# Relational graph convolution, gathered half: nine of a group's 18 edge tiles counted from its first edge, nine from its end

## The chip, the cores and the metric

The kernel runs on one core of one Trainium2 chip. The metric is the device time of one execution in microseconds (us), the median of several runs. "Edge tile" below means 128 consecutive edges; TensorE, VectorE, ScalarE, GpSimd and SyncE (SP, which issues most transfers) are the core's engines, in the profile PE, DVE, ACT, POOL and SP.

## The reference, cut to what matters

Two graph networks follow one another on N = 3125 nodes and E = 103125 edges, which are sorted by destination (50000 random edges, their reverses, and one loop for each node, so 33 edges a node on average).

```python
h = relu(layernorm(x));  x = x + gcn(h)          # 4 convolutions, hidden width 256
h = relu(layernorm(x));  x = x + rgcn(h)         # 3 layers, width 128, R = 16 relations

def rgcn_layer(x, src, tgt, edge_type, W, root, bias):
    seg = tgt * R + edge_type
    agg = segment_sum(x[src], seg, N * R)                     # a sum for each node and relation
    cnt = segment_sum(ones, seg, N * R)
    agg = agg / clip(cnt, 1)
    return einsum('nrd,rdo->no', agg, W) + x @ root + bias    # relu between layers
```

The change is in the second network: in how the edges of a node are brought to the sums `agg`.

## The kernel before, in words

The program has three parts.

**Index part** (`index_edges`). It packs each edge's destination, type and source in one word (`c_d`), finds by counting where each node's edges begin (`s_d`), and checks the assumptions that the rest rests on. The check ends in one flag (L618), on which all engines branch: to `regular`, or to a slow general path.

**First network.** Seven column blocks of an adjacency matrix (`adj_d`, q = 0 to 6, 512 nodes each) are built by TensorE, then multiplied with the features in four stages. In each stage `stream(q)` (L1205, on SP) loads a block and `aggregate` (L827) runs 75 or 150 matmuls over it; two buffers hold blocks. While this runs, smaller pieces of work that the second network needs are spread among the matmuls as generators. In the third such stage the generator is `relation_tiles` (steps taken in `between`), together with `residual` (L1327 to L1334) and `first_rows`, which finish x for the nodes of the block before.

**Second network** (`rgcn_mixed`). Nodes are handled in 25 blocks of 128, each for three layers. A block has two groups of GR = 64 nodes. The first half of a block takes its messages from features held on chip: one-hot matrices G (L1596) pick them with TensorE (L1621), ScalarE copies them out of PSUM (L1623), and matmuls with the one-hot S sum them by node and relation (L1688, L1692). The second half is the **gathered half**, group 2b + 1: GpSimd fetches the source rows with one indirect transfer for each edge tile (`msg`, L1518; 20 buffers), VectorE makes a one-hot `sel` from the tile's keys (L1637, six tiles an instruction), and TensorE multiplies (L1651), three times for each tile, since features are held as a sum of three bf16 terms. `plans` gives how many tiles go with each of a block's six batches; within a block these matmuls lie between those of the first half. VectorE scales the sums by 1 / cnt (`scaled`, L1512) into `gs`, and `project` (L1526, L1528) applies the relation weights.

A group has about 64 x 33 = 2112 edges. The kernel gives it TR = 18 tiles, which start at the group's first edge. Which nodes can occur in tile k isn't known when the program is built, so `windows` gives each tile an interval of nodes that its edges can belong to: where node n begins lies within five standard deviations of 33 n. The interval widens with the distance from the group's first edge. Its width sets the width of `sel` and the columns of L1651: (nodes in the window) x 16 relations. A group's sums lie in two PSUM tiles, one for 32 nodes each (half h = 0 and 1); a tile whose window crosses node 32 needs matmuls for both. `touched` lists the tiles of each half.

```python
found.append((lo, hi))             # windows(): node range of tile k, counted from the group's first edge
...
a0, a1 = max(lo, 32 * h), min(hi + 1, 32 * h + 32)       # rgcn_mixed: columns of half h
```

`relation_tiles` prepares this once. `gathered_words` loads every group's first edge number into `at` (L738, 18 small loads on SP, one for each tile), adds 128 k (L739) and fetches the words (`w`, L742, seven indirect transfers). `relative` makes node numbers relative to the group (L751, L752), L1241 subtracts the window's first node, and `to_edges` turns the results so that edges lie on partitions (L762, TensorE transposes), for the relative node `rel`, the type `typ` and the source. From these come the keys `key2` (L1248) and the sources `src_t` (L1251). Then one-hots `hr` and `ht` (L812) and small matmuls (L1275) count the edges by node and relation; these also use the windows.

The order of instructions on each engine is set when the program is built, by a scheduler that can move an instruction ahead of others that it doesn't depend on; what comes first in the program isn't always first on an engine.

Of the kernel before, what the change touches and what calls it, by code (L numbers as in the profile page):

```python
# [21 lines left out]
P = 128  # L22
N = 3125
# [19 lines left out]
GA, TA, CA = 8, 3, 13  # L43
RA = 32 * TA
IA = NB * GA
GR, TR, CR = 64, 18, 7
RR = 7 * TR
NGR = CR * 7
# [5 lines left out]
def windows(size, tiles):  # L54

    found = []
    for k in range(tiles):
        lo = max(n for n in range(size) if 33 * n + 5 * math.sqrt(32 * n) <= P * k)
        hi = min([n for n in range(size) if 33 * (n + 1) - 5 * math.sqrt(32 * (n + 1)) >= P * (k + 1)] + [size - 1])
        found.append((lo, hi))  # L60
    return found


def bounds(win, size, tiles):

    lows, highs = {}, {}
    for k, (lo, hi) in enumerate(win):
        highs[lo] = min(highs.get(lo, tiles * P), P * k)
        if hi < size - 1:
            lows[hi + 1] = max(lows.get(hi + 1, 0), P * (k + 1))  # L70
    return lows, highs


WIN = windows(GR, TR)
WINA = windows(GA, TA)


# [358 lines left out]
def index_edges(tc, keep, a, c_d, s_d, h_d, dinv, flag):  # L436


    nc = tc.nc
    with ExitStack() as x:  # L440
        prep = x.enter_context(tc.tile_pool(name="ix", bufs=1))
# [133 lines left out]

        wide = 2 * GR + 1
        g_i = prep.tile([NGR, GR + 1], I32, name="g_i")
        nc.sync.dma_start(g_i[:, :GR], s_d[: NGR * GR].rearrange("(g e) o -> g (e o)", e=GR))  # L580
        nc.sync.dma_start(g_i[:, GR:], s_d[GR: (NGR + 1) * GR].rearrange("(g e) o -> g (e o)", e=GR)[:, :1])
# [1 line left out]
        high = prep.tile([NGR, wide], F32, name="high")  # L583
        nc.vector.memset(low, 0.0)
        nc.vector.memset(high, float(TR * P))
        for o, step, size, (lows, highs) in ((0, GR, GR, bounds(WIN, GR, TR)),
                                              (GR + 1, GA, GR, bounds(WINA, GA, TA))):
            for t, values in ((low, lows), (high, highs)):
                for n, v in values.items():
                    nc.gpsimd.memset(t[:, o + n:o + size:step], float(v))  # L590
        g_f = prep.tile([NGR, wide], F32, name="g_f")
        nc.vector.tensor_copy(g_f[:, :GR + 1], g_i)
        nc.vector.tensor_copy(g_f[:, GR + 1:], g_i[:, :GR])
        g_r = prep.tile([NGR, wide], F32, name="g_r")
        nc.vector.tensor_scalar(g_r[:, :GR + 1], g_f[:, :GR + 1], g_f[:, :1], None, op0=ALU.subtract)
        g_e = g_f[:, GR + 1:].rearrange("p (g e) -> p g e", e=GA)
        nc.vector.tensor_tensor(g_r[:, GR + 1:].rearrange("p (g e) -> p g e", e=GA), g_e,
                                g_e[:, :, :1].to_broadcast([NGR, GR // GA, GA]), op=ALU.subtract)
        more = prep.tile([NGR, wide], F32, name="more")
        nc.vector.tensor_scalar(more, g_f, float(E), None, op0=ALU.is_lt)  # L600
# [40 lines left out]
def regular(ctx: ExitStack, tc: tile.TileContext, a: dict, out: bass.AP, c_d, s_d, h_d, dinv):  # L641
# [45 lines left out]
    with ExitStack() as gx:  # L687
# [24 lines left out]
        def gathered_words(pool, rows_, tiles, groups, cols, size):  # L712
# [12 lines left out]
            nc.vector.tensor_copy(k_f, k_i)  # L725
            p_f = pool.tile([n, 1], F32, name="p_f")
            nc.vector.tensor_copy(p_f, p_i)
            g_f = pool.tile([n, 1], F32, name="g_f")
            nc.vector.scalar_tensor_tensor(g_f, k_f, -float(groups), p_f, op0=ALU.mult, op1=ALU.add)
            nc.vector.tensor_scalar(g_f, g_f, float(size), None, op0=ALU.mult)  # L730
            nc.vector.tensor_scalar(k_f, k_f, float(P), None, op0=ALU.mult)
            base = pool.tile([n, cols], F32, name="base")
            iota(nc, base, [[size * groups, cols]])
            nc.vector.tensor_scalar(base, base, g_f, None, op0=ALU.add)
            at = pool.tile([n, cols], I32, name="at")
            first = s_d[: cols * groups * size].rearrange("(c g e) o -> g c (e o)", c=cols, g=groups)[:, :, 0]
            for k in range(tiles):
                nc.sync.dma_start(at[k * groups:(k + 1) * groups, :], first)  # L738
            nc.vector.tensor_scalar(at, at, k_f, None, op0=ALU.add)  # L739
            w = pool.tile([n, cols, P], I32, name="w")  # L740
            for c in range(cols):
                nc.gpsimd.indirect_dma_start(out=w[:, c, :], out_offset=None, in_=c_d,  # L742
                                             in_offset=bass.IndirectOffsetOnAxis(ap=at[:, c:c + 1], axis=0))
            return w, base

        def relative(pool, w, base):

# [474 lines left out]
        def relation_tiles():  # L1222

            with tc.tile_pool(name="tr", bufs=1) as tr:
                rel2 = tr.tile([P, CR * RR, 2], F16, name="rel2")
                typ2 = tr.tile([P, CR * RR, 2], F16, name="typ2")
                with tc.tile_pool(name="trw", bufs=1) as tw:
                    w, at = gathered_words(tw, RR, TR, 7, CR, GR)
                    yield

                    rel, d_i = relative(tw, w, at)
                    lo_f = tw.tile([RR, 1], F32, name="lo_f")
                    nc.vector.memset(lo_f, 0.0)
                    p_f = tw.tile([RR, 1], F32, name="pr_f")
                    iota(nc, p_f, [[0, 1]], 1)
                    more = tw.tile([RR, 1], F32, name="more")
                    for k in range(1, TR):
                        nc.vector.tensor_scalar(more, p_f, 7.0 * k, float(WIN[k][0] - WIN[k - 1][0]),
                                                op0=ALU.is_ge, op1=ALU.mult)
                        nc.vector.tensor_add(lo_f, lo_f, more)  # L1240
                    nc.vector.tensor_scalar(rel, rel, lo_f, 100.0, op0=ALU.subtract, op1=ALU.min)  # L1241
                    to_edges(tw, rel, RR, CR, dup(rel2, 1))
                    typ = tw.tile([RR, CR, P], F32, name="typ")
                    nc.vector.tensor_scalar(d_i, w, 12, NR - 1, op0=ALU.logical_shift_right, op1=ALU.bitwise_and)
# [496 lines left out]
```

## Time and profile before

| | |
|---|---|
| median of 3 runs | 2903.13 us (2902.95 to 2910.56) |
| profiled execution, its own time | 3358.47 us |
| its span, first to last instruction | 3356.6 us |
| second network, in the span | 1105 to 3357 us |
| PE busy, whole span | 2812.2 us (84%) |
| PE busy 1105 to 1815 us | 629.8 of 710 us |
| mean granted clock of TensorE | 0.935 |
| L1651 PE | 4536 matmuls, 10% of the chain of waits |
| L1518 POOL | 1296 gathers, 1051 ns each |
| L1637 DVE | 216 one-hots, 917 ns each |
| L738 SP, third stage | 18 loads in 6.38 us |

The profiled execution is 455 us longer than the median of the runs. Its durations are those of one execution; busy shares are averages over stages that differ, so each part of the work is to be looked up in its own stretch of the timeline. In a row of the groups of instructions, the numbers after the bar are busy us, mean ns of one, and the engine's idle time just before them, with what ended it. In a row of the timeline, the columns are start, us, engine, line, operation, out<-in, count, and in brackets the idle time before it.

### The profile page before, as it was taken

Reading aid. Unit: us, or ns where it says so; the run is one execution under the profiler, and the core shown is the slowest. Engines: PE = TensorE matmul, PEld = TensorE weight load, DVE = VectorE, ACT = ScalarE, POOL = GpSimd, SP = SyncE. Lnnn points to the kernel's source line nnn. Section 1 sums busy time; section 2 is a strip of 40 time slices with the busy share of each in tenths; the row PEclk is TensorE's granted clock in tenths of the full one; section 3 lists DMA queues with packets and bytes.
Section 4 is the critical chain, followed back from the end, with each engine's and each line's share of the span. In section 5 each row is a group of like instructions: output and inputs, shape, how many; then the busy total and the mean of one; then the engine's idle time right before and its main releaser. Section 6 shows DMA issues by size and latency. Waiting matters only on the chain.

```text
span 3356.6 us, 62945 instructions
## 1 busy us (share of the span) xinstructions
PE 2812.2 (84%) x25471; PEld 1869.7 (56%) x25712; DVE 1750.0 (52%) x3711; ACT 1136.3 (34%) x2747; POOL 1426.7 (43%) x1418
## 2 busy tenths in 40 slices
PE   0577899999986898889898788888889788888888
PEld 0344454555543566666665565666656466566656
DVE  6899765766463444444444344444444344444443
ACT  0455422222212343333333233333434233333333
POOL 4000000000002566666663566566663656666663
PEclk9988899999997899999999899999989799899999
DMA  5111322222244344444444344444443344344441
GB/s 161 55 79 79 129 79 80 90 80 80 100 161 147 111 131 127 125 132 130 133 125 111 105 128 126 123 131 122 132 119 98 107 121 128 117 124 125 128 126 59
DMA packets 186848, 383.08 MB, mean 114 GB/s; under 512 B 59589, under 2 KB 137652, under 8 KB 183474
## 3 DMA queue, kind: packets, MB, share of 16 engines
q1 hardware_dynamic: 111474, 234.68, 21.2%
q0 software_dynamic: 65456, 135.18, 14.4%
q10 hardware_dynamic: 9616, 9.08, 1.0%
q8 instruction: 203, 3.33, 0.4%
q14 instruction: 99, 0.81, 0.1%
HBM read 346.51 MB, written 32.30 MB: 113 GB/s over the span
## 4 chain that ended last, share of the span: by engine, by line
PE 71%; DVE 12%; issue 10%; DMA 3%; another core or an unknown queue 2%; ACT 2%; POOL 1%; DVEq 0%; SPq 0%; ACTq 0%; POOLq 0%
PE p_p L1688 19%; PE p_a L827 12%; PE p_g L1621 11%; PE p_a L1651 10%; PE p_m L1528 8%; PE p_p L1692 3%; DVE gs L1512 2%; PE p_a L892 2%; DVE ov L812 1%; DVE ou L812 1%; PE p_m L845 1%; PE p_b L915 1%; DMA seg<-f_d,at_i 1%; ACT m L1623 1%
## 5 line engine op out<-in xcount | busy, mean ns | idle before, releaser
L1518 POOL DMA_INDIRECT msg<-tab,src_t x1296 | 1361.5, 1051 | 799.4 <-PE p_a L1651 284.4
L1623 ACT CAST m<-p_g 128x384 bf16<-128x384 f32 x1800 | 769.5, 490 | 912.5 <-PE p_g L1621 387.8
L1688 PE MATMUL p_p<-S,m 128*128 128x256 bf16 x5184 | 699.3, 286 | 96.5 <-DVE gs L1512 37.3
L1688 PEld LDWEIGHTS <-m 128*128 128x128 bf16 x5400 | 520.0, 102 | 323.0 <-issue 239.5
L1651 PE MATMUL p_a<-sel,msg 128*128 128x144 bf16 (+9 forms) x4536 | 422.3, 240 | 55.4 <-issue 49.8
L1600 DVE TENSOR_TENSOR S<-iota_k,key_s 128x1536 bf16<-128x1536 f16 x300 | 287.4, 958 | 334.3 <-PE p_g L1621 125.8
L1651 PEld LDWEIGHTS <-msg 128*128 128x128 bf16 x4536 | 350.8, 99 | 132.9 <-issue 86.9
L1596 DVE TENSOR_TENSOR G<-sr,pid 128x768 bf16<-128x768 f16 x300 | 166.4, 555 | 495.3 <-PE p_g L1621 254.9
L1621 PE MATMUL p_g<-X,G 128*32 128x384 bf16 x4800 | 317.5, 344 | 77.9 <-issue 62.7
L1621 PEld LDWEIGHTS <-G 128*32 128x32 bf16 x7200 | 183.1, 96 | 354.8 <-issue 299.7
L827 PE MATMUL p_a<-adj,x3a 128*128 128x512 bf16 (+1 forms) x1531 | 316.3, 358 | 7.8 <-DMA adj<-adj_d 4.3
L1528 PE MATMUL p_m<-gs,Wr 128*128 128x256 f32 (+2 forms) x1344 | 274.9, 363 | 20.5 <-issue 14.7
L1512 DVE TENSOR_TENSOR gs<-p_a,wv 128x512 f32<-128x512 f32 x150 | 156.5, 1044 | 259.2 <-PE p_p L1688 112.6
L1528 PEld LDWEIGHTS p_m<-gs,Wr 128*128 128x128 f32 x1344 | 240.8, 197 | 48.6 <-issue 15.2
L1637 DVE TENSOR_TENSOR sel<-iota_k,key 128x1248 bf16<-128x1248 f16 (+2 forms) x216 | 198.0, 917 | 132.1 <-PE p_a L1651 73.1
L827 PEld LDWEIGHTS <-x3a 128*128 128x128 bf16 x1575 | 143.8, 98 | 149.0 <-issue 7.6
L827 PE MATMUL p_a<-adj,x3b 128*128 128x512 bf16 (+1 forms) x1023 | 209.1, 355 | 1.3
L1621 PE MATMUL p_g<-Xn,G 128*32 128x384 bf16 x2400 | 158.9, 344 | 43.8 <-issue 24.4
L915 PE MATMUL p_b<-ov,ou 128*128 128x150 f16 (+1 forms) x1200 | 115.3, 245 | 56.7 <-DVE ou L812 34.9
L1512 DVE TENSOR_TENSOR gs<-p_p,wv 128x512 f32<-128x512 f32 x144 | 149.6, 1039 | 12.6 <-PE p_p L1692 10.4
L827 PEld LDWEIGHTS <-x3b 128*128 128x128 bf16 x1050 | 95.6, 98 | 95.0
L1529 ACT ACTIVATE xT<-p_m,bias 128x256 f32<-128x256 f32 (+2 forms) x42 | 18.8, 448 | 382.1 <-PE p_g L1621 243.0
(386 smaller groups left out, 2320.9 us busy)
## 6 DMA issues: line engine op xcount, KB each, us to landing
wv<-winv_d SPq DMA_DIRECT2D x147, 512.0 KB
adj<-adj_d SPq DMA_DIRECT2D x18, 3200.0 KB
sr<-slots_d SPq DMA_DIRECT2D x75, 768.0 KB
msg<-tab,src_t POOLq DMA_INDIRECT x1296
adj_d<-adj SPq DMA_DIRECT2D x6, 3200.0 KB
tab<-X SPq DMA_DIRECT2D x50, 96.0 KB
adj<-adj_d SPq DMA_DIRECT2D x3, 800.0 KB
cv<-codes_d SPq DMA_DIRECT2D x75, 32.0 KB
```

Of the source, the lines that this page charges most:

```text
L827: nc.tensor.matmul(p[k][:, :n], x3_[:, i, s, k * P:(k + 1) * P], adj[:, i, :n], start=(i == 0 and s == 0), stop=(i == NB - 1 and s == 2))
L915: nc.tensor.matmul(pb[:, gg * IA + lo * NB:gg * IA + (hi + 1) * NB], hot_u[k][:, g + gg, :], hot_v[k][:, g + gg, :(hi + 1 - lo) * NB], sta ...
L1512: nc.vector.tensor_tensor(gs[:, :, n0:n0 + 32].rearrange("p r n -> p n r"), p.rearrange("p (n r) -> p n r", r=NR), wv.rearrange("p (n r) - ...
L1518: nc.gpsimd.indirect_dma_start(out=m.rearrange("p s d -> p (s d)"), out_offset=None, in_=table, in_offset=bass.IndirectOffsetOnAxis(ap=at, ...
L1528: nc.tensor.matmul(po[:, :n], W[:, r, :], gs[:, r, o:o + n], start=False, stop=(r == NR - 1))
L1596: nc.vector.tensor_tensor(G.rearrange("p (c w) -> p c w", w=2), sr[:, q, :].rearrange("p (c w) -> p c w", w=2), pid[:, None, :].to_broadca ...
L1600: nc.vector.tensor_tensor(S[q].rearrange("p j (c w) -> p j c w", w=2), iota_k[:, :GS * NR].rearrange("p (c w) -> p c w", w=2)[:, None, :, ...
L1621: nc.tensor.matmul(pg[o:o + 32, :3 * D], w, X[:, i, :, :].rearrange("p s d -> p (s d)"), start=True, stop=True)
L1623: nc.scalar.copy(m[:, tiles.index(t), :], pg[:, :3 * D])
L1637: nc.vector.tensor_tensor(s6[:, :, :n6].rearrange("p j (c w) -> p j c w", w=2), iota_k[:, :n6].rearrange("p (c w) -> p c w", w=2)[:, None, ...
L1651: nc.tensor.matmul(pa[h][:, (a0 - 32 * h) * NR:(a1 - 32 * h) * NR], msgs[k][:, i, :], s6[:, k % 6, (a0 - lo) * NR:(a1 - lo) * NR], start=( ...
L1688: nc.tensor.matmul(pb[t // 12][:, o:o + GS * NR], m[:, n, i * D:(i + 1) * D], hot, start=(t % 12 == 0 and i == 0), stop=False, skip_group_ ...
```

## The change

Tiles 0 to 8 of a group keep their place: 128 k edges from the first edge. Tiles 9 to 17 are counted back from the group's end, so that tile 17 holds its last 128 edges; their windows are those of tiles 8 to 0, mirrored. The two sets overlap in most groups, so the edges of the later set that the first nine tiles already hold are masked: `lim` says how many lanes of a tile those are, and `rel` of these is raised by 200, which no window reaches. For this `gathered_words` loads the beginnings of the next group for the later tiles, and the group's own beginnings once more (`begin`, 18 loads). Nodes past the last are taken as having 33 edges each (`far`, `behind`), and the index check covers both sets of windows.

```diff
@@ module level
-WIN = windows(GR, TR)
+WINH = windows(GR, TR)[:TR // 2]
+WIN = WINH + [(GR - 1 - hi, GR - 1 - lo) for lo, hi in reversed(WINH)]
@@ index_edges
-        wide = 2 * GR + 1
+        wide = 3 * GR + 2
+        ends = 2 * GR + 1
...
-        for o, step, size, (lows, highs) in ((0, GR, GR, bounds(WIN, GR, TR)),
+        for o, step, size, (lows, highs) in ((0, GR, GR, bounds(WINH, GR, TR)),
                                               (GR + 1, GA, GR, bounds(WINA, GA, TA))):
             for t, values in ((low, lows), (high, highs)):
                 for n, v in values.items():
                     nc.gpsimd.memset(t[:, o + n:o + size:step], float(v))
+        for t, values in zip((low, high), bounds(WINH, GR, TR)):
+            for n, v in values.items():
+                nc.gpsimd.memset(t[:, ends + GR - n:ends + GR - n + 1], float(v))
+
+        behind = prep.tile([NGR, GR + 1], F32, name="behind")
+        nc.gpsimd.iota(behind, pattern=[[33, GR + 1]], base=-33 * N, channel_multiplier=33 * GR,
+                       allow_small_or_imprecise_dtypes=True)
+        nc.gpsimd.tensor_scalar(behind, behind, 0.0, None, op0=ALU.max)
         g_f = prep.tile([NGR, wide], F32, name="g_f")
-        nc.vector.tensor_copy(g_f[:, :GR + 1], g_i)
-        nc.vector.tensor_copy(g_f[:, GR + 1:], g_i[:, :GR])
+        nc.vector.tensor_tensor(g_f[:, :GR + 1], g_i, behind, op=ALU.add)
+        nc.vector.tensor_copy(g_f[:, GR + 1:ends], g_i[:, :GR])
+        nc.vector.tensor_copy(g_f[:, ends:], g_f[:, :GR + 1])
         g_r = prep.tile([NGR, wide], F32, name="g_r")
...
+        nc.vector.tensor_scalar(g_r[:, ends:], g_f[:, :GR + 1], g_f[:, GR:GR + 1], -1.0, op0=ALU.subtract,
+                                op1=ALU.mult)
@@ gathered_words (head is len(WINH) for the relation tiles, None for the other caller)
-            first = s_d[: cols * groups * size].rearrange("(c g e) o -> g c (e o)", c=cols, g=groups)[:, :, 0]
+            first, after = (s_d[o: o + cols * groups * size].rearrange("(c g e) o -> g c (e o)", c=cols, g=groups)
+                            [:, :, 0] for o in (0, 0 if head is None else size))
             for k in range(tiles):
-                nc.sync.dma_start(at[k * groups:(k + 1) * groups, :], first)
-            nc.vector.tensor_scalar(at, at, k_f, None, op0=ALU.add)
+                nc.sync.dma_start(at[k * groups:(k + 1) * groups, :],
+                                  first if head is None or k < head else after)
+            if head is None:
+                nc.vector.tensor_scalar(at, at, k_f, None, op0=ALU.add)
+            else:
+                tail = pool.tile([n, 1], F32, name="tail")
+                nc.vector.tensor_scalar(tail, p_f, float(head * groups), None, op0=ALU.is_ge)
+                nc.vector.scalar_tensor_tensor(k_f, tail, -float(tiles * P), k_f, op0=ALU.mult, op1=ALU.add)
+                far = pool.tile([n, cols], F32, name="far")
+                nc.vector.tensor_scalar(far, base, float(size - N), 0.0, op0=ALU.add, op1=ALU.max)
+                nc.vector.tensor_scalar(far, far, 33.0, tail, op0=ALU.mult, op1=ALU.mult)
+                nc.vector.tensor_tensor(at, at, far, op=ALU.add)
+                nc.vector.tensor_scalar(at, at, k_f, 0.0, op0=ALU.add, op1=ALU.max)
+                begin = pool.tile([n, cols], I32, name="begin")
+                for k in range(tiles):
+                    nc.sync.dma_start(begin[k * groups:(k + 1) * groups, :], first)
+                lim = pool.tile([n, cols], F32, name="lim")
+                nc.vector.tensor_tensor(lim, begin, at, op=ALU.subtract)
+                nc.vector.tensor_scalar(lim, lim, float(head * P), tail, op0=ALU.add, op1=ALU.mult)
@@ relation_tiles
-                    w, at = gathered_words(tw, RR, TR, 7, CR, GR)
+                    w, at, lim = gathered_words(tw, RR, TR, 7, CR, GR, len(WINH))
...
+                    typ = tw.tile([RR, CR, P], F32, name="typ")
+                    nc.vector.tensor_tensor(typ, iota_k[:RR, None, :P].to_broadcast([RR, CR, P]),
+                                            lim[:, :, None].to_broadcast([RR, CR, P]), op=ALU.is_lt)
+                    nc.vector.scalar_tensor_tensor(rel, typ, 200.0, rel, op0=ALU.mult, op1=ALU.add)
                     nc.vector.tensor_scalar(rel, rel, lo_f, 100.0, op0=ALU.subtract, op1=ALU.min)
                     to_edges(tw, rel, RR, CR, dup(rel2, 1))
-                    typ = tw.tile([RR, CR, P], F32, name="typ")
```

More of the change, by code (lines that the diff above doesn't have):

```diff
@@ L590, in index_edges @@
                     nc.gpsimd.memset(t[:, o + n:o + size:step], float(v))
+        for t, values in zip((low, high), bounds(WINH, GR, TR)):
[5 more added lines that the diff above has]
+        nc.gpsimd.tensor_scalar(behind, behind, 0.0, None, op0=ALU.max)
         g_f = prep.tile([NGR, wide], F32, name="g_f")
-        nc.vector.tensor_copy(g_f[:, :GR + 1], g_i)
-        nc.vector.tensor_copy(g_f[:, GR + 1:], g_i[:, :GR])
+        nc.vector.tensor_tensor(g_f[:, :GR + 1], g_i, behind, op=ALU.add)
+        nc.vector.tensor_copy(g_f[:, GR + 1:ends], g_i[:, :GR])
+        nc.vector.tensor_copy(g_f[:, ends:], g_f[:, :GR + 1])
         g_r = prep.tile([NGR, wide], F32, name="g_r")
         nc.vector.tensor_scalar(g_r[:, :GR + 1], g_f[:, :GR + 1], g_f[:, :1], None, op0=ALU.subtract)
-        g_e = g_f[:, GR + 1:].rearrange("p (g e) -> p g e", e=GA)
-        nc.vector.tensor_tensor(g_r[:, GR + 1:].rearrange("p (g e) -> p g e", e=GA), g_e,
+        nc.vector.tensor_scalar(g_r[:, ends:], g_f[:, :GR + 1], g_f[:, GR:GR + 1], -1.0, op0=ALU.subtract,
+                                op1=ALU.mult)
+        g_e = g_f[:, GR + 1:ends].rearrange("p (g e) -> p g e", e=GA)
+        nc.vector.tensor_tensor(g_r[:, GR + 1:ends].rearrange("p (g e) -> p g e", e=GA), g_e,
                                 g_e[:, :, :1].to_broadcast([NGR, GR // GA, GA]), op=ALU.subtract)
@@ L710, in regular, with gathered_words @@
         u2 = fk.tile([P, CA * RA, 2], F16, name="u2")
-        def gathered_words(pool, rows_, tiles, groups, cols, size):
+        def gathered_words(pool, rows_, tiles, groups, cols, size, head=None):
             n = rows_
@@ L743, in gathered_words @@
                                              in_offset=bass.IndirectOffsetOnAxis(ap=at[:, c:c + 1], axis=0))
-            return w, base
+            return (w, base) if head is None else (w, base, lim)
         def relative(pool, w, base):
```

## The prediction

> **What bounds the kernel now.** I read the page first: engine shares, then the chain of waits.
>
> ```profile
> span 3356.6 us, 62945 instructions
> PE 2812.2 (84%) x25471; PEld 1869.7 (56%) x25712; DVE 1750.0 (52%) x3711; ACT 1136.3 (34%) x2747; POOL 1426.7 (43%) x1418
> PE 71%; DVE 12%; issue 10%; DMA 3%; another core or an unknown queue 2%; ACT 2%; POOL 1%; DVEq 0%; SPq 0%; ACTq 0%; POOLq 0%
> ```
>
> TensorE carries 71% of the chain; the page's next line gives L1651, the matmuls whose windows change, 10% of it. VectorE is on it for 12%, GpSimd for 1%. The groups of instructions then give the counts of what the change touches:
>
> ```profile
> L1518 POOL DMA_INDIRECT msg<-tab,src_t x1296 | 1361.5, 1051 | 799.4 <-PE p_a L1651 284.4
> L1651 PE MATMUL p_a<-sel,msg 128*128 128x144 bf16 (+9 forms) x4536 | 422.3, 240 | 55.4 <-issue 49.8
> L1637 DVE TENSOR_TENSOR sel<-iota_k,key 128x1248 bf16<-128x1248 f16 (+2 forms) x216 | 198.0, 917 | 132.1 <-PE p_a L1651 73.1
> ```
>
> L1651 runs 63 times in each of 72 blocks (24 gathered groups by 3 layers): 21 pairs of tile and half, three splits each. Its 240 ns is the length of one pipelined matmul, not its price. The price is the distance between starts, which TensorE's timeline of one full-speed stretch gives:
>
> ```profile
> 2209.88 0.71 PE L1651 MATMUL p_a<-sel,msg 128*128 128x192 bf16 x9
> 2210.52 0.83 PE L1621 MATMUL p_g<-Xn,G 128*32 128x384 bf16 x14
> ...
> 2220.45 1.24 PE L1651 MATMUL p_a<-sel,msg 128*128 128x192 bf16 x15
> 2221.53 0.67 PE L1526 MATMUL p_m<-xT,root 128*128 128x256 f32 x2
> ...
> 2231.13 1.48 PE L1651 MATMUL p_a<-sel,msg 128*128 128x96 bf16 x18
> 2232.44 0.27 PE L1535 MATMUL p_m<-ident,xT 128*128 128x128 f32 x1
> ```
>
> The 15 are tiles 4 to 7 (832 columns, three splits, 2,496): from 2220.45 to the next group at 2221.53 is 1.08 us, 0.43 ns a column. The 18 are tiles 8 to 11 (2,976 columns): 1.31 us, 0.44 ns. Matmuls of 32 to 272 columns are mixed here, so no floor for short ones shows.
>
> The other place is the third stage of the first network (L1205, L827, q = 0 and 1), where the words of the relation tiles are fetched. All engines, in order of time:
>
> ```profile
> 929.21 0.63 DVE L751 TENSOR_SCALAR d_i<-w 126x896 int32<-126x896 int32 x1 [9.88 <-DMA w<-c_d,at]
> 929.87 1.09 DVE L752 TENSOR_TENSOR rel<-d_i,base 126x896 f32<-126x896 int32 x1
> 931.00 0.69 DVE L1241 TENSOR_SCALAR rel<-rel,lo_f 126x896 f32<-126x896 f32 x1
> 931.60 0.62 DVE L1244 TENSOR_SCALAR d_i<-w 126x896 int32<-126x896 int32 x1
> 931.80 0.29 PEld L762 LDWEIGHTS p_b<-ident,rel 126*128 126x128 f32 x2 [8.62 <-issue]
> 931.83 0.45 PE L762 MATMUL p_b<-ident,rel 126*128 126x126 f32 x1 [8.16 <-DVE rel L1241]
> ```
>
> TensorE stands 8.16 us for rel; VectorE before that 9.88 us for w. Whatever is put between w and rel lengthens a wait that is already bare.
>
> **What the Trainium skill says.** "TensorE: Matmul & The Clock Gate", section "Wait — 56ns, not 53.3ns?": a warm matmul starts every N / 2.4 GHz plus about 2.5 ns, never under 25 ns. The trace agrees: 0.43 ns a column over mixtures against 0.417 plus the fixed part. Same page, "What's actually happening": the array runs at half clock after an idle window. The trace agrees: the page's clock row dips to 7 and below, mean 0.935. Same page, "Architectural detail: the array is 16× 32×32, not 1× 128×128": weight loads are pulled ahead of matmuls under way; so the loads that come with extra matmuls should cost nothing (PEld is busy 56%). "SBUF — State Buffer", "Who interferes with whom": GpSimd is shut out while VectorE runs a two-port operation. Gathers here last from 0.94 to 1.71 us in one 12 us stretch; the cause of the spread isn't shown.
>
> **The change part by part.** The windows follow from the diff's arithmetic. Tiles 0 to 8 are unchanged. Nodes in tiles 9 to 17: before 15, 16, 16, 16, 17, 16, 12, 9, 5; after 15, 14, 13, 13, 12, 11, 10, 9, 6.
>
> (1) *L1651 columns.* Per group 225 nodes by 16 relations, 3,600 columns, become 206 by 16, 3,296. Times three splits: 912 columns fewer per block. By 72 blocks: 65,664. At 0.417 ns: 27.4 us; at 0.44 ns: 28.9. I take −28. Tile 10 now touches both halves: 22 pairs, so 3 more matmuls and loads a block, 216 in all; at about 2.5 ns 0.5 us, inside the rounding. In the changed program's instruction order TensorE's sequence in this stage is otherwise the same, and GpSimd's 1,296 gathers stay.
>
> (2) *sel on VectorE (L1637).* The three widths of a block go from 1,248, 1,536, 1,632 elements to 1,248, 1,440, 1,248. By form they took 809, 951 and 990 ns; 1,440 is then about 905. Saved: 46 + 181 = 227 ns a block, 16 us in all. VectorE is busy some 44% of that stage, so hidden: 0. It could shorten TensorE's 37 us of waits for gs (L1512), which queue behind sel: 0 to −5, I take 0.
>
> (3) *Index check (L578 to L618).* GpSimd's added memsets, iota and maximum precede its first gather at 22.11 us; it stands idle 19.0 us there: 0. On VectorE, between g_i's landing (64.13) and the flag (66.78): one more copy (0.18), one more subtraction (0.25), and four operations over 194 instead of 129 columns (together about 0.2). All engines branch on that flag: +0.6.
>
> (4) *Third stage, the words.* In the changed order, `at` gets one more operation after its landing (+0.4, row of 0.22 us plus its wait). Then, between rel (L752) and rel − lo (L1241), VectorE now has: the seven x_sb additions (L1328) moved ahead, six of 0.60 and one of 0.25, 3.9; residual and its statistics for q = 0 (L1331, L669), 2.1; one moved shift, 0.65; lim, two small ones, 0.35; the comparison and the masked addition over 126x896, each like L752's 1.09, 2.2; scraps 0.4. Sum 9.6, with `at` 10.0. So rel's transposes start at about 941.8 instead of 931.8. The whole of q = 1 (75 matmuls) is now queued on TensorE behind them and behind those of typ and src; before, some 15 matmuls filled the gaps. That fill was largely q = 0's and q = 1's own work and is not lost, but TensorE's stand grows from 8.2 to about 17 us plus some 2 us between transposes: +10. Back come the VectorE waits later in the stage (a few of 0.2 to 0.9 us in q = 1 and 2), since the additions are done: −2. I take +8, bounds +4 and +14.
>
> (5) *SP's queue.* 18 more loads (`begin`) at about 0.35 us each (18 `at` took 6.38 us). Four go before x_sb, fourteen after, and adj of q = 1, issued at 910.68 before, goes behind all. x_sb's two loads are issued 915.71 to 922.23; some `begin` wait for its landing; the last by about 927.5, adj at 928. The chain shows 11.8 us for such a load: landed by 940, q = 1 wants it at about 949. Cover 9 us: 0; were q = 1 not late by (4), this would itself cost about 5. `begin` lands before lim is due (about 938): 0.
>
> Sum: −28 + 0.6 + 8 = −19.4. The profiled execution's own time is 3358.5 us (span 3356.6): 3339 after. The median shown is 2903.1, 455 less; TensorE's "issue" waits (10% of the span, 340 us) and half-clock stretches behind them are the likely surplus. Columns and VectorE's operations don't depend on that, so I carry the microseconds over: 2883.7.
>
> **The rivals.**
>
> (A) *GpSimd sets the pace in the timed runs; slower.* For it: a block needs 18 gathers by 1.05 + 0.30 us (the gap between back-to-back gathers), 24.3 us at the mean, 22.5 at the shortest; TensorE's work in a block at full speed comes to about 22.6, plus 0.8 of waits for VectorE and ScalarE. Against it: TensorE waited only 1.3 us in all for msg, and the edge buffers made GpSimd wait 284 us. If gathers take above about 1.27 us on average in an unprofiled run, the columns saved buy nothing: +8.6, 2912.
>
> (B) *Half is given back.* The shorter L1651 brings TensorE earlier to gs and m, which come at VectorE's and ScalarE's pace (37 and 27 us of such waits now): −14 + 8.6, 2898.
>
> (C) *The stage loss is double* (adj of q = 1 late as well): −28 + 20, 2895.
>
> (D) The check trips and the general path runs: several times the time. The drawn edges keep every bound of the new windows, worked out from the reference's inputs: 1%.
>
> **How the numbers follow.** About 0.3% (8.7 us) can be told from no change. Likeliest case 62%: 2884, own range 2874 to 2893. (B) 20%, a quarter of it still beyond 8.7 us; (A) 12%, mostly over the bound; (C) 5%. Faster 0.67, same 0.22, slower 0.11. The range reaches to (B) and (C) and to the clock's upper bound (65,664 columns at 0.935 clock and sel's 5 us: −34, with a stage loss of +4): 2870 to 2905.
>
> **What would show it.** Right: L1651 x4752 with its chain share near 9.4%; its 15-to-18 groups at 0.43 to 0.44 ns a column; sel about 840 ns mean; a block pair about 0.8 us shorter; TensorE's wait for rel 16 to 18 us and q = 1 ending about 8 us later. Wrong: PE waiting for msg by tens of microseconds (A); waits for gs growing by over 10 us (B); q = 1 waiting for adj (C).

## The result, and the profile after

The changed kernel takes **2913.77 us** (median of 20 runs, 2903.17 to 2920.23), the kernel before 2903.04 (20 runs, 2900.05 to 2911.85). The ratio is 1.0034, 95% interval 1.0026 to 1.0042: slower by 10.7 us, where 19 faster had been forecast. The profiled execution after has a span of 2908.0 us and lies with its timed runs; that of the kernel before had taken 3358 us, so its profile was taken again (e1, below), and "before" from here on means that one: span 2904.7, own time 2906.5.

The page of the changed kernel, its span, its engines and its chain:

```profile
span 2908.0 us, 63660 instructions
...
PE 2621.6 (90%) x25928; PEld 1790.6 (62%) x25928; DVE 1735.8 (60%) x3722; ACT 1107.0 (38%) x2747; POOL 1408.6 (48%) x1424
...
PE 72%; DMA 13%; DVE 10%; issue 2%; POOL 1%; ACT 1%; DVEq 0%; SPq 0%; POOLq 0%; ACTq 0%
PE p_p L1724 17%; PE p_a L860 15%; PE p_g L1657 10%; DMA msg<-tab,src_t 9%; PE p_m L1564 9%; PE p_a L1687 9%; PE p_p L1728 3%; PE p_a L925 2%; DVE ov L845 2%; DVE ou L845 2%; PE p_m L878 1%; PE p_b L948 1%; PE p_g L1701 1%; DMA seg<-f_d,at_i 1%; PE p_m L1562 1%
```

The chain has "DMA msg" on it with 9%, as much as the matmuls that were made cheaper (L1687 is L1651 of before). The costliest groups of the same page (columns: busy, mean ns, then the engine's idle time just before them and what ended it):

```profile
L1554 POOL DMA_INDIRECT msg<-tab,src_t x1296 | 1342.6, 1036 | 403.8 <-issue 97.8
...
L1687 PE MATMUL p_a<-sel,msg 128*128 128x144 bf16 (+6 forms) x4752 | 379.9, 229 | 56.4 <-DMA msg<-tab,src_t 55.9
L1687 PEld LDWEIGHTS <-msg 128*128 128x128 bf16 x4752 | 330.2, 98 | 109.9 <-DMA msg<-tab,src_t 71.0
```

The columns went (L1687 is busy 380 us, its like in e1 405), and TensorE waits for msg in their place: 56 us on the matmuls, 71 us on their weight loads. The two rows show the same stretches of time, so they don't add up; TensorE stands 71 us for msg. In the trace, 1299 of the 1303 gaps between GpSimd's gathers in the second network are 0.4 us or less, nearly all 0.30: it gathers without a pause, except for two stops of 35 us where a layer ends. That is the picture that rival A of the prediction draws; the experiments test it.

The third stage lost what the prediction said. VectorE there, by time (start, length, and in brackets the idle time before):

```profile
928.00 0.63 DVE L784 TENSOR_SCALAR d_i<-w 126x896 int32<-126x896 int32 x1 [8.92 <-DMA w<-c_d,at]
928.66 1.09 DVE L785 TENSOR_TENSOR rel<-d_i,base 126x896 f32<-126x896 int32 x1
929.67 0.68 DVE L1364 TENSOR_TENSOR x_sb<-x_sb,r_L_gnn_b 128x512 f32<-128x512 f32 x1
...
936.09 0.16 DVE L771 TENSOR_TENSOR lim<-begin,at 126x7 f32<-126x7 int32 x1
936.28 0.23 DVE L772 TENSOR_SCALAR lim<-lim,tail 126x7 f32<-126x7 f32 x1
936.55 1.09 DVE L1275 TENSOR_TENSOR typ<-iota_k,lim 126x896 f32<-126x896 f16 x1
...
937.68 1.09 DVE L1277 SCALAR_TENSOR_TENSOR rel<-typ,rel 126x896 f32<-126x896 f32 x1
...
938.94 0.68 DVE L1278 TENSOR_SCALAR rel<-rel,lo_f 126x896 f32<-126x896 f32 x1
```

TensorE, which waits for the last of these:

```profile
939.77 1.70 PE L795 MATMUL p_b<-ident,rel 126*128 126x126 f32 x7 [14.15 <-DVE rel L1278]
```

Between the first use of w and rel's transposes lie 11.8 us; in the kernel before (e1) these matmuls start 2.6 us after it:

```profile
932.49 1.71 PE L762 MATMUL p_b<-ident,rel 126*128 126x126 f32 x7 [8.21 <-DVE rel L1241]
```

The last wide at_s copy of the stage moves from 1042.05 to 1050.32 and the first gather of the second network from 1061.63 to 1069.89, both by 8.3 us. The gather, in e1 and then in the changed kernel:

```profile
1061.63 0.95 POOL L1518 DMA_INDIRECT msg<-tab,src_t  x1 [0.30 <-issue]
```

```profile
1069.89 0.95 POOL L1554 DMA_INDIRECT msg<-tab,src_t  x1 [0.30 <-issue]
```

### The profile page after: what moved, and what is told of

Same layout as the page of the kernel before. It is cut to its first block, busy times and chain, and to the rows that moved or that the text cites. A ratio compares the mean times of both kernels' runs of the same rounds, so it can differ in the third digit from the quotient of the medians.

```text
span 2908.0 us, 63660 instructions
## 1 busy us (share of the span) xinstructions
PE 2621.6 (90%) x25928; PEld 1790.6 (62%) x25928; DVE 1735.8 (60%) x3722; ACT 1107.0 (38%) x2747; POOL 1408.6 (48%) x1424
## 4 chain that ended last, share of the span: by engine, by line
PE 72%; DMA 13%; DVE 10%; issue 2%; POOL 1%; ACT 1%; DVEq 0%; SPq 0%; POOLq 0%; ACTq 0%
PE p_p L1724 17%; PE p_a L860 15%; PE p_g L1657 10%; DMA msg<-tab,src_t 9%; PE p_m L1564 9%; PE p_a L1687 9%; PE p_p L1728 3%; PE p_a L925 2%; DVE ov L845 2%; DVE ou L845 2%; PE p_m L878 1%; PE p_b L948 1%; PE p_g L1701 1%; DMA seg<-f_d,at_i 1%; PE p_m L1562 1%
## 5 line engine op out<-in xcount | busy, mean ns | idle before, releaser
L1554 POOL DMA_INDIRECT msg<-tab,src_t x1296 | 1342.6, 1036 | 403.8 <-issue 97.8
L1659 ACT CAST m<-p_g 128x384 bf16<-128x384 f32 x1800 | 737.8, 494 | 419.5 <-PE p_g L1657 412.0
L1724 PE MATMUL p_p<-S,m 128*128 128x256 bf16 x5184 | 644.2, 274 | 0.0
L1724 PEld LDWEIGHTS <-m 128*128 128x128 bf16 x5400 | 492.2, 98 | 188.3 <-issue 134.8
L1687 PE MATMUL p_a<-sel,msg 128*128 128x144 bf16 (+6 forms) x4752 | 379.9, 229 | 56.4 <-DMA msg<-tab,src_t 55.9
L1687 PEld LDWEIGHTS <-msg 128*128 128x128 bf16 x4752 | 330.2, 98 | 109.9 <-DMA msg<-tab,src_t 71.0
L1657 PE MATMUL p_g<-X,G 128*32 128x384 bf16 x4800 | 261.2, 331 | 3.9 <-DVE G L1632 3.4
L1657 PEld LDWEIGHTS <-G 128*32 128x32 bf16 x7200 | 158.4, 96 | 164.5 <-issue 87.1
L1673 DVE TENSOR_TENSOR sel<-iota_k,key 128x1248 bf16<-128x1248 f16 (+1 forms) x216 | 179.6, 831 | 126.6 <-PE p_a L1687 122.1
```

Source lines behind the costliest of these rows:

```text
L1554: nc.gpsimd.indirect_dma_start(out=m.rearrange("p s d -> p (s d)"), out_offset=None, in_=table, in_offset=bass.IndirectOffsetOnAxis(ap=at, ...
L1657: nc.tensor.matmul(pg[o:o + 32, :3 * D], w, X[:, i, :, :].rearrange("p s d -> p (s d)"), start=True, stop=True)
L1659: nc.scalar.copy(m[:, tiles.index(t), :], pg[:, :3 * D])
L1673: nc.vector.tensor_tensor(s6[:, :, :n6].rearrange("p j (c w) -> p j c w", w=2), iota_k[:, :n6].rearrange("p (c w) -> p c w", w=2)[:, None, ...
L1687: nc.tensor.matmul(pa[h][:, (a0 - 32 * h) * NR:(a1 - 32 * h) * NR], msgs[k][:, i, :], s6[:, k % 6, (a0 - lo) * NR:(a1 - lo) * NR], start=( ...
L1724: nc.tensor.matmul(pb[t // 12][:, o:o + GS * NR], m[:, n, i * D:(i + 1) * D], hot, start=(t % 12 == 0 and i == 0), stop=False, skip_group_ ...
```

## The experiments

The theories were **G**: GpSimd's gathers set the pace of the second network, before and after, so that fewer columns only make TensorE wait longer; **T**: TensorE sets the pace and the gain was lost elsewhere. Later **L**: a gather is shut out while a VectorE comparison with both inputs in SBUF runs; **M**: its length comes from memory traffic or a busy VectorE in general.

### e1: the kernel before, profiled again

No edit.

> The kernel before, unchanged, for a profile of an ordinary execution (the first one took 3358 us of its own where the runs take 2903). Theory G (GpSimd's 18 gathers a block set the pace of the second network, in the kernel before too): own time near 2903; TensorE waits for msg by some tens of microseconds, perhaps 60 to 110 on L1651's matmuls and weight loads together; almost every gap between two gathers of the second network is 0.30 us; a block pair takes about as long as in the changed kernel, 48.3 us, within 0.3. Theory T (TensorE sets the pace, the gain was lost elsewhere): waits for msg of a few microseconds, block pair about 0.8 us longer than in the changed kernel. In both theories TensorE's wait for rel in the third stage is about 8 us and the stage's last at_s copy (L831) stands some 9 us earlier than in the changed kernel.

2906.53 us. Its page:

```profile
span 2904.7 us, 62945 instructions
...
PE 2628.6 (90%) x25471; PEld 1800.7 (62%) x25712; DVE 1750.3 (60%) x3711; ACT 1107.2 (38%) x2747; POOL 1406.3 (48%) x1418
...
PE 75%; DVE 11%; DMA 9%; issue 3%; ACT 1%; POOL 1%; DVEq 0%; ACTq 0%; POOLq 0%; SPq 0%
PE p_p L1688 19%; PE p_a L827 14%; PE p_g L1621 11%; PE p_a L1651 10%; PE p_m L1528 9%; DMA msg<-tab,src_t 5%; PE p_p L1692 3%; PE p_a L892 2%; DVE ov L812 2%; DVE ou L812 2%; PE p_m L845 1%; PE p_b L915 1%; DMA seg<-f_d,at_i 1%; PE p_g L1665 1%; PE p_m L1526 1%
...
L1518 POOL DMA_INDIRECT msg<-tab,src_t x1296 | 1340.1, 1034 | 405.5 <-issue 104.2
...
L1651 PE MATMUL p_a<-sel,msg 128*128 128x144 bf16 (+9 forms) x4536 | 405.3, 238 | 36.4 <-DMA msg<-tab,src_t 36.3
L1651 PEld LDWEIGHTS <-msg 128*128 128x128 bf16 x4536 | 341.6, 98 | 96.6 <-DMA msg<-tab,src_t 47.6
```

The profile that the prediction was made from gave issue 10% and no msg among the lines that its page lists of the chain; here it is issue 3% and msg 5%, and TensorE already stands 48 us for msg (36 us on L1651's matmuls, within the 48 on its weight loads; the 60 to 110 us expected counted both). 1299 of 1303 gaps of GpSimd are short, as after; in the 3358 us execution 251 were longer. G's signs are there, and T's are not: a block pair takes 48.5 us on average here and 48.6 after (32 intervals between the starts of project, each).

### e2 and e3: the columns alone, back and away

e2 widens the changed kernel's tail windows; e3 narrows those of the kernel before and leaves its preparation alone.

```
# e2, on the changed kernel
-WIN = WINH + [(GR - 1 - hi, GR - 1 - lo) for lo, hi in reversed(WINH)]
+WIN = WINH + [(23, 37), (25, 40), (32, 47), (36, 51), (40, 56), (44, 59), (49, 60), (53, 61), (58, 63)]
# e3, on the kernel before; bounds() goes on using WINC
-WIN = windows(GR, TR)
+WINC = windows(GR, TR)
+WIN = WINC[:9] + [(30, 44), (33, 46), (37, 49), (41, 53), (44, 55), (48, 58), (52, 61), (55, 63), (58, 63)]
```

> The changed kernel with its nine tail windows widened to the widths of before (226 nodes a group, 3,616 columns in place of 3,296); preparation and gathers as in the changed kernel. Theory G: the extra 69,120 columns are paid out of TensorE's waits for msg: 2914, within 4 us of the changed kernel, and those waits shrink from 127 us to some 90 to 105. Theory T: 29 us slower than the changed kernel, 2943.

> The preparation of before, the third stage and the index check included, with the narrow windows of the changed kernel (3,296 columns a group instead of 3,600, 21 pairs). Edges that fall outside the narrow windows are left out of the sums. This is the column saving alone, without its price. Theory G: 2903, between 0 and 4 us below the kernel before. Theory T: 28 us below it, 2875.

e2: 2899.35 us (0.9983, 0.9976 to 0.9990 of before). e3: 2909.39 (1.0016, 1.0010 to 1.0023). T is out: with 69,120 more columns the kernel gets 14 us faster than the changed one, with 65,664 fewer it gets 5.5 us slower than before. G's size was off too: it gave at most 4 us either way, and in e2 the waits for msg fell to 64 us by the expectation's count, not to 90 to 105. The gathers say why. e2, then e3:

```profile
L1554 POOL DMA_INDIRECT msg<-tab,src_t x1296 | 1329.2, 1026 | 405.5 <-PE p_a L1687 94.5
```

```profile
L1519 POOL DMA_INDIRECT msg<-tab,src_t x1296 | 1350.4, 1042 | 403.8 <-PE p_a L1652 94.5
```

Against the changed kernel's 1036 ns, 1296 gathers of 1026 are 13 us less; against e1's 1034, 1042 are 10 us more. In e3 some of that comes back, since GpSimd's stops at the layer ends are 7.5 us shorter than in e1: from the first gather to the last it takes 3 us longer. Where GpSimd is the bound, the length of its gathers goes into the time, and that length changes with the windows though the gathers do not.

### Why a gather lasts 0.94 or 1.66 us

GpSimd's timeline in the changed kernel, then VectorE's over the same stretch:

```profile
2020.07 0.94 POOL L1554 DMA_INDIRECT msg<-tab,src_t  x1 [0.30 <-PE p_a L1687]
...
2023.80 1.53 POOL L1554 DMA_INDIRECT msg<-tab,src_t  x1 [0.30 <-PE p_a L1687]
2025.64 0.95 POOL L1554 DMA_INDIRECT msg<-tab,src_t  x1 [0.30 <-PE p_p L1724]
...
2028.14 1.66 POOL L1554 DMA_INDIRECT msg<-tab,src_t  x1 [0.30 <-PE p_a L1687]
```

```profile
2019.85 1.05 DVE L1548 TENSOR_TENSOR gs<-p_p,wv 128x512 f32<-128x512 f32 x1
...
2023.70 0.81 DVE L1673 TENSOR_TENSOR sel<-iota_k,key 128x1248 bf16<-128x1248 f16 x1 [1.81 <-PE p_a L1687]
...
2025.79 0.96 DVE L1636 TENSOR_TENSOR S<-iota_k,key_s 128x1536 bf16<-128x1536 f16 x1 [0.19 <-PE p_p L1724]
...
2028.07 0.91 DVE L1673 TENSOR_TENSOR sel<-iota_k,key 128x1440 bf16<-128x1440 f16 x1
```

Take the four gathers in turn. At 2020.07 gs is running, whose one input lies in PSUM: 0.94. At 2023.80 a sel is 0.10 us old and has 0.71 to go: 0.945 + 0.71 - 0.126 = 1.53. At 2025.64 VectorE is idle, and an S that begins 0.15 us later does no harm: 0.95. At 2028.14 a sel has 0.84 to go: 1.66. Counted over the whole trace, 375 gathers began while S, sel or G ran, and 290 of them lasted over 20 ns more than 945. Of the 85 that did not, 57 began within 34 ns of the comparison's start and 28 with at most 0.15 us of it to go. Of the 921 other gathers 5 were stretched, all beside GV, one more comparison with both inputs in SBUF; of the 149 that began beside gs none was. Of the stretched ones, the excess is the remaining time of that VectorE instruction less 125 ns (123 to 130 for the middle 80%). The excess is 118 us in all: S 56, sel 54, G 7, the rest 1. In e1 it is 115, in e2 105, in e3 126.

The Trainium skill has the rule, in "SBUF — State Buffer", section "Who interferes with whom": a VectorE instruction with two SBUF inputs contends with a GpSimd instruction that reads SBUF, and one with at most one SBUF input, outside the two-port modes, does not. The trace agrees (gs against S, sel and G). That it is the reading of the gather's indices, early in it, which is shut out would also fit the harmless S at 2025.79, and the 57: the G among them took about 0.60 us where their median is 0.56, as if the gather had come first. This is argued, not shown.

### e4 and e5: 15 gathers a group

```
-msgs = [gather(...) for k in range(TR if two else 0)]
+msgs = [gather(...) for k in range(TR - 3 if two else 0)]
+msgs += msgs[TR - 6:]
```

> The kernel before with 15 gathers a group instead of 18; tiles 15 to 17 take the messages of tiles 12 to 14 a second time, so their edges are left out of the sums. All matmuls and VectorE's operations stay. Theory G (GpSimd's gathers set the pace): GpSimd needs 15 x 1.335 = 20 us a block and TensorE sets the pace at 23.4: a block pair falls from 48.3 to about 46.8 us, in all -54: about 2850. Theory T (TensorE sets the pace already): within 6 us of 2904.

> The changed kernel with the same 15 gathers a group. Theory G: TensorE sets the pace here too, and now the 65,664 fewer columns count: 28 us less than the kernel before with 15 gathers, and 9 us of the third stage back on top: 17 to 20 us faster than that kernel, about 2832. Theory T: as far above the kernel before with 15 gathers as the changed kernel is above the kernel before, some 10 us.

2855.18 us (0.9826, 0.9809 to 0.9842 of before) and 2836.68 (0.9771, 0.9754 to 0.9787). G's numbers hold to about 5 us: 50 us from three gathers less, and 18.5 between the two where the changed kernel with 18 gathers is 10.7 behind. TensorE's waits for msg, in e4 and then in e5 (total, times, longest):

```profile
PE p_a L1652 <- DMA msg<-tab,src_t: 1.2, 3, 0.7
```

```profile
PE p_a L1688 <- DMA msg<-tab,src_t: 3.0, 3, 1.5
```

A block pair takes 46.95 us in e4 and 46.23 in e5: 0.72 us, near the 0.8 that the prediction gave for the columns. These two leave out transfers as well as GpSimd's time; e13 to e15 keep every transfer.

### e8: S and sel against numbers in PSUM

```
-ps_g = rx.enter_context(tc.tile_pool(name="ps_g", bufs=4, space=PSUM))
+ps_g = rx.enter_context(tc.tile_pool(name="ps_g", bufs=3, space=PSUM))
+iota_w = rx.enter_context(tc.tile_pool(name="ps_i", bufs=1, space=PSUM)).tile([P, GS * NR // 2], F32, name="iota_q")
+nc.vector.tensor_copy(iota_w, iota_k[:, :GS * NR].bitcast(F32))
+iota_q = iota_w.bitcast(F16)
...
-  iota_k[:, :GS * NR]    # S      -> iota_q[:, :GS * NR]
-  iota_k[:, :n6]         # sel    -> iota_q[:, :n6]
```

(The text on record says 512 numbers; GS x NR is 256.)

> The changed kernel with the 512 numbers that S and sel compare against read from PSUM instead of SBUF (one of TensorE's four p_g banks is given up for them); all 18 gathers stay. In the traces a gather that starts while a 16-bit comparison (S, sel, G: both inputs in SBUF) is running lasts 945 ns plus that comparison's remaining time less 126 ns, and one that starts beside gs (one input in PSUM) or an idle VectorE lasts 945. Theory L (a comparison with both inputs in SBUF shuts a starting gather out): S and sel no longer stretch any, only G does; the mean gather falls from 1036 to 950 to 975 ns, GpSimd's need to 22.5 to 23 us a block, and TensorE sets the pace: 50 to 90 us faster than the changed kernel. Theory M (the stretch comes from memory or DMA traffic, or from VectorE being busy at all): mean gather stays at 1020 to 1045, time within 10 us. Against L only in its size: reading PSUM may make S and sel slower, and three p_g banks may hold TensorE up.

3004.96 us (1.0348, 1.0331 to 1.0366): slower by 91 us than the changed kernel, while L's own sign came out. Gathers fell to 954 ns, and none of the 350 that began beside S or sel was stretched. S took 957 ns as before, so PSUM as a source costs VectorE nothing. The chain shows where the time went:

```profile
PE 77%; DVE 10%; ACT 6%; DMA 4%; issue 2%; POOL 0%; ACTq 0%; DVEq 0%; SPq 0%; POOLq 0%
PE p_p L1727 20%; PE p_a L860 14%; PE p_g L1660 12%; PE p_a L1690 10%; PE p_m L1567 9%; ACT m L1662 5%; PE p_p L1731 3%; PE p_a L925 2%; DVE ov L845 2%; DVE ou L845 1%; PE p_m L878 1%; PE p_b L948 1%; PE p_g L1704 1%; DMA seg<-f_d,at_i 1%; PE p_m L1565 1%
```

ScalarE's copies m out of p_g are on it with 5%, and msg has left it: with three p_g banks TensorE runs into the copies (its matmuls into p_g wait 19.9 us for m, in 111 waits, against 0.2 in the changed kernel). How the rest of the loss comes about was not taken apart.

e9, the same edit on the kernel before, has no time: its widest sel compares against 272 numbers, of which the edit put 256 into PSUM.

### e10 to e12: the numbers in an unused part of the p_m bank

p_m uses 256 of its bank's 512 columns, so there is room without giving up a bank. e10 makes this edit on the changed kernel, e11 on the kernel before, e12 on e10 together with e6's edit (below).

```
+bank = ps_m.tile([P, 512], F32, name="p_m")
+nc.vector.tensor_copy(bank[:, 376:], iota_k[:, :272].bitcast(F32))
+iota_q = bank[:, 376:].bitcast(F16)
...
-po = ps_m.tile([P, 512], F32, name="p_m")      (pt in the same way)
+po = bank[:, :256]
```

S and sel read iota_q as in e8.

> As the changed kernel with S's and sel's numbers in PSUM, but kept in the unused quarter of the p_m bank, so that TensorE keeps its four p_g banks. Theory L (the gathers' stretch, and through it the pace of the second network, comes from comparisons with both inputs in SBUF): mean gather 950 to 960 ns, GpSimd's need 18 x 1.255 = 22.6 us a block, TensorE's 22.9: a block pair falls from 48.3 to 45.8 to 46.4 us and the time to that of the changed kernel with 15 gathers, 2825 to 2845. If the three banks were not what cost the kernel with the separate bank its 100 us (PSUM reads disturb TensorE themselves): about 3000 again.

> The same edit to the kernel before. Theory L: mean gather 950 to 975 ns; TensorE sets the pace with its 3,600 columns a group: near the kernel before with 15 gathers, 2850 to 2865, and 17 to 22 us slower than the changed kernel with this edit (28 us of columns, less 9 of the third stage). Against L: as slow as or slower than before.

> Both mends on the changed kernel: S's and sel's numbers in the unused quarter of the p_m bank, and the begin loads on ScalarE's queue beside at's. If the two losses are independent: 6 to 7 us faster than the changed kernel with the first mend alone, about 2828, and the fastest of all that were run with their whole computation.

These three ran on a chip where the kernel before itself takes 3355.1 us (51 runs, 3336 to 3378): the condition that the first profile of before was taken in. e10 took 3367.74 (1.0028, 1.0012 to 1.0043), e11 3367.32 (1.0041, 1.0025 to 1.0057), e12 3352.70 (1.0002, 0.9983 to 1.0021). e10's chain:

```profile
PE 75%; DVE 11%; issue 8%; DMA 2%; another core or an unknown queue 2%; ACT 1%; POOL 1%; DVEq 0%; ACTq 0%; POOLq 0%; SPq 0%
```

TensorE waits for issue, GpSimd has slack (339 gaps over 0.4 us), and shorter gathers buy nothing. Two of the numbers stay unexplained: e11 is 12 us behind the kernel before, though it differs from it by this edit alone, and e12 is 15 us ahead of e10 where 6 to 7 were expected. The theories are decided only where the other runs were made.

### e13 to e15: the same three kernels on a chip of the first kind

> The changed kernel with S's and sel's numbers in the unused quarter of the p_m bank, again, on a chip where the kernel before takes about 2904 us (the first time the chip was one on which it takes 3355, TensorE waiting for issue). Theory L: mean gather 950 to 960 ns, TensorE no longer waits for msg, a block pair of 45.8 to 46.4 us, 2825 to 2845 us. If PSUM reads disturb TensorE: near 3000.

> The kernel before with the same edit, again. Theory L: 2850 to 2865 us, 17 to 22 us slower than the changed kernel with this edit, since TensorE's columns now count.

> The changed kernel with both mends, again. If the two losses are independent: 6 to 7 us faster than with the first mend alone, about 2828.

e13, changed kernel: 2838.83 us (0.9772, 0.9753 to 0.9790 of before). e14, kernel before: 2860.76 (0.9842, 0.9825 to 0.9860). e15: 2832.86 (0.9749, 0.9731 to 0.9767), the fastest of all. Groups of e13:

```profile
L1557 POOL DMA_INDIRECT msg<-tab,src_t x1296 | 1246.7, 962 | 405.8 <-PE p_a L1690 95.6
...
L1639 DVE TENSOR_TENSOR S<-p_m,key_s 128x1536 bf16<-128x1536 f16 x300 | 285.9, 953 | 152.8 <-PE p_p L1727 134.5
L1690 PE MATMUL p_a<-sel,msg 128*128 128x144 bf16 (+6 forms) x4752 | 368.9, 229 | 6.4 <-DMA msg<-tab,src_t 6.4
```

And of e14, the kernel before with the same edit:

```profile
L1521 POOL DMA_INDIRECT msg<-tab,src_t x1296 | 1251.8, 966 | 419.8 <-PE p_a L1654 115.8
...
L1654 PE MATMUL p_a<-sel,msg 128*128 128x144 bf16 (+9 forms) x4536 | 397.7, 237 | 6.0 <-DMA msg<-tab,src_t 6.0
```

GpSimd's timeline in e13, and VectorE's:

```profile
2002.04 1.32 POOL L1557 DMA_INDIRECT msg<-tab,src_t  x1 [0.30 <-PE p_g L1660]
2003.66 0.95 POOL L1557 DMA_INDIRECT msg<-tab,src_t  x1 [0.30 <-PE p_g L1660]
...
2007.42 0.95 POOL L1557 DMA_INDIRECT msg<-tab,src_t  x1 [0.30 <-PE p_g L1704]
```

```profile
2002.01 0.54 DVE L1635 TENSOR_TENSOR G<-sr,pid 128x768 bf16<-128x768 f16 x1
...
2003.49 0.80 DVE L1676 TENSOR_TENSOR sel<-p_m,key 128x1248 bf16<-128x1248 f16 x1
...
2007.21 0.89 DVE L1676 TENSOR_TENSOR sel<-p_m,key 128x1440 bf16<-128x1440 f16 x1
```

The two gathers that begin beside a sel with 0.63 and 0.68 us to go take 0.95; the one beside G, whose inputs both still lie in SBUF, is stretched by 0.38. M is out: VectorE is as busy as ever, and its operations are the same but for where one input lies. Of the 317 gathers that began beside S or sel none was stretched. TensorE's waits for msg fell from 71 to 8 us (on the matmuls alone from 56 to 6.4), and now the columns count: e13 is 22 us ahead of e14, a block pair 46.3 against 47.1. GpSimd's gaps are as short as before (1297 of 1303), so short gaps alone don't tell which engine sets the pace; TensorE's waits do.

The free corner has a price in order: in e13 and e14 none of the 516 comparisons that read it runs at the same time as a matmul into p_m, while in e1 60 of the same 516 did.

### e6: the begin loads on ScalarE's queue

```
 for k in range(tiles):
     nc.sync.dma_start(at[...], ...)
+    if head is not None:
+        nc.scalar.dma_start(begin[k * groups:(k + 1) * groups, :], first)
...
-begin = pool.tile([n, cols], I32, name="begin")        # moved ahead of the loop
-for k in range(tiles):
-    nc.sync.dma_start(begin[k * groups:(k + 1) * groups, :], first)
```

> The changed kernel with its 18 begin loads on ScalarE's queue, issued beside the at loads, so that lim is ready before w lands, x_sb's additions no longer stand ahead of rel in VectorE's order, and q = 1's adj is loaded early. Between rel and rel - lo are left the d_i shift, the comparison and the masked addition, about 2.8 us. If step 4 of the prediction has the mechanism of the lost 9 us right: 5 to 7 us faster than the changed kernel, about 2908, still 3 to 5 above before. If the loss has another cause (the later SP loads, the index check): within 2 us of the changed kernel.

2907.25 us (1.0011, 1.0001 to 1.0021 of before): 6.5 us faster than the changed kernel. TensorE's wait for rel falls from 14.15 us to:

```profile
936.41 1.70 PE L796 MATMUL p_b<-ident,rel 126*128 126x126 f32 x7 [9.63 <-DVE rel L1279]
```

x_sb's additions have gone back behind rel, and the first gather begins at 1063.63, 2.0 us after e1's instead of 8.3. e15 against e13 gives the same 6.0 us a second time, with the other loss taken away.

## Why the prediction was wrong, point by point

**The step that failed is how the sum was carried over: the -28 of step (1) was counted as time.** "Columns and VectorE's operations don't depend on that, so I carry the microseconds over." The number of columns doesn't depend on the execution; whether they are on the path does. The profile of before came from an execution in which TensorE lost some 340 us to issue, and there GpSimd had time to spare. In the runs that were to be forecast it had none: its 18 gathers need 24.0 us a block, TensorE's work 23.5 before and 23.1 after (half a block pair of e4 and e5). The saved columns turned into waits: TensorE stands 71 us for msg where it stood 48.

**(1) was right in size where TensorE is the bound.** Between e14 and e13 lie 22 us although e13's first gather comes 9.4 us later (1070.7 against 1061.3): 31 us. Between e4 and e5: 18.5 + 9 (the first gather moves from 1061.7 to 1070.7) = 27.5. With 18 stretched gathers it is worth less than nothing: -28 turned into about +2 (10.7 measured less 8.3 of preparation), and the columns alone (e3) cost 5.5.

**Rival A was the outcome**: 2912 said, 2913.77 measured, at a chance of 12%. Its arithmetic held: 18 x (1.036 + 0.30) = 24.0 us a block against 24.3 measured. The two reasons given against it, waits for msg of 1.3 us and 284 us in which GpSimd waited for buffers, were both products of the slow TensorE of that one execution: in e1 TensorE stands 48 us for msg, and only 4 of GpSimd's 1303 gaps are over 0.4 us. Rival A took the gather's length as given, 1.05 us; that a change of windows moves it by 10 ns, and so the time by 13 us, was nowhere in the prediction.

**(2) sel, "hidden: 0", failed too.** VectorE's time was hidden, as stated, but its comparisons reach the path through GpSimd: not by how long VectorE is busy, but by how much of a comparison is left when a gather begins. That is a matter of phase, which I can't compute from a profile; in sum e2's gathers are 13 us shorter than the changed kernel's, e3's 10 us longer than e1's. The prediction had the spread of the gathers' lengths before it, and cited the section that holds the rule, but took from it only the two-port operations, not the two SBUF inputs.

**(3)** +0.6 forecast; the flag (ix_flag) comes 0.08 us later (67.22 against 67.14).

**(4)** +8 forecast, 8.3 measured, in part by luck. The order of VectorE's instructions was as read from the changed program. But rel's matmuls come at 939.77 instead of 941.8: w came 1.2 us earlier than in the profile that the sum was made from (928.00 against 929.21), where 0.4 later had been put down, and 11.8 us instead of 12.2 lie between. So TensorE's wait is 14.15 us instead of 17, 6 more than in e1. What seems to have made up for it has no term in the sum: from the transposes on, TensorE's granted clock (its share of full speed) was 0.50 from 939.8 to 950 us and 0.96 from 950 to 960, in e1 0.62 from 932.5 to 940 and 1.00 from there. By an estimate from these shares that costs 5.5 us of TensorE's time after and 2.8 before. The prediction names the half clock after an idle stretch, reads it from a clock row whose lowest digit is 7, and puts no price on it.

**(5)** 0 forecast for the longer SP queue. TensorE's only wait for adj in the changed kernel, 4.2 us, has its like in e1 with 4.3. The load of adj was issued at 928.37, as forecast. But the queue was not free of effect: e6 shows that with begin issued earlier and on another queue VectorE's order is better and 6.5 us come back.

**Rivals B, C and D** did not occur: no new waits for gs or m, no doubled stage loss, no general path.

## What to carry to other kernels

When the profiled execution is far from the runs it is to forecast, its waits are not theirs: look for the second slowest engine, compute its need per block from counts, durations and gaps alone (here 18 x 1.335 = 24.0 us against TensorE's 23.5), and ask for a profile near the median before costing anything. With the two engines within a few per cent of each other, a saving on the faster one was worth nothing here; what it is worth was seen only after the other had been relieved. And where GpSimd's gathers are the bound, look at which VectorE instructions run when they start: moving one input of two comparisons to a free corner of PSUM was worth 45 us on the kernel before and 75 on the changed one, though 12 us were lost by it on the chip where TensorE waits for issue (e11).

## What the runs showed of the hardware that I had not expected

- A gather of 128 rows of 768 bytes takes 945 ns plus a gap of 0.30 us, and is stretched by what remains, less about 126 ns, of a comparison with both inputs in SBUF that had been running for more than some 30 ns when it began; not by one that begins after it, and not by an instruction with one input in PSUM.
- VectorE's 16-bit comparison runs as fast with one input in PSUM (S 953 ns) as with both in SBUF (960).
- Fewer columns made the kernel slower and more columns made it faster (e2, e3), with gathers that were 10 us longer and 13 us shorter in sum.
- With three PSUM banks for p_g the kernel takes 166 us more than with four (e8 3004.96, e13 2838.83; both have S and sel read PSUM, e8 from a bank of their own).
- Chips differ. On one, the kernel before takes 3355 us in 51 runs, with TensorE waiting for issue; on others, 2903 to 2905.5 (the medians of four sets of runs). Why TensorE's instructions come late there is open.
